# Layer 1's experts in pairs with their weights applied before the last matrix, and layer 3's matrices loaded during the edge loop

## The chip, the cores and the metric

The kernel runs on one core of a Trainium2 chip. The metric is the time of one execution on the device in microseconds (us). The engines are PE (matrix products; PEld is its loading of the stationary operand), DVE, ACT and POOL for element work, and SP, which only issues transfers; ACT and POOL issue transfers as well, each on a queue of its own.

## What is computed

The program is a graph network of four layers on 3125 nodes with 256 features and 103,125 edges. Each layer adds a graph attention, a linear attention and then a feed-forward block to x. The change touches two feed-forward blocks. Layer 1 has a shared network of three matrices and four experts of three matrices, of which the two best count for a node:

```
xn = layernorm(x)
shared = relu(relu(xn @ sW1 + sb1) @ sW2 + sb2) @ sW3 + sb3      # 256 -> 256 -> 128 -> 256
for e in 4 experts:
    o[e] = relu(relu(xn @ eW1[e] + eb1[e]) @ eW2[e] + eb2[e]) @ eW3[e] + eb3[e]   # 256 -> 128 -> 64 -> 256
wf = weights of the top 2 of softmax(xn @ gW + gb), 0 elsewhere
x = x + shared + sum over e of wf[:, e] * o[e]
```

Layer 3 sends each node to one of eight experts: a common hidden layer of 1024 (W1, gelu), a gate on it, and then the matrix Wd[e] (1024 x 256) of the best expert, with bias bd[e], times its probability, added to x.

## The kernel before

Nodes lie in 25 tiles of 125 (TP); a group is four or three tiles (GROUPS: four groups of 4, three of 3), so a product has 500 or 375 columns. All values are float32. The Tile framework orders the instructions on each engine and gives out the buffers of each pool; only in the blocks under `manual_schedule` are PE and DVE kept in the order written. `self.mm(p, pairs)` adds up products in one PSUM tile; since it is a helper, its products are line 716 whatever they compute, and the names of the tiles tell them apart.

**Layer 1, `ffn1`.** `before(i)` transposes a group's xn to xT (line 288), computes the four gate scores (p_score) and the weights wf by `softmax` and `top2`, and is called one group ahead. For a group the kernel computes the shared network (s1 and s2 into p_tr, then for each tile p_y = h2 with s3, plus a product of one row with the bias sb3) and adds it to x on DVE (line 1060). For each expert, e1 goes into p_tr and ACT makes h1e from it (line 1065), e2 into p_e, 64 rows high, and ACT makes h2e (line 1069). Then for each tile a product with e3 goes into p_y, and DVE multiplies it by the node's weight and adds it to x (line 1073). At the end `add_weighted_biases` transposes wf tile by tile (line 707), copies it (709), multiplies it by the biases eb3 (711) and adds (712). p_tr, p_e and p_y have two buffers each.

**Layer 3.** `edge_attention` is a loop of 101 steps of eight columns of 128 edges. In a step SP loads row, ef and mask for two steps ahead, POOL gathers eight times 128 rows into z_edge (line 1930, three buffers), DVE and ACT compute the weights, and PE sums them up (p_acc, line 1998). Twice in a step `piece()` takes one piece of other work from a list: first all pieces of `mix3` (the linear attention, which reads xn and xT), then those of `hidden3`, one generator for each entry of ENDS once the node tiles of that entry are done. `hidden3` writes the hidden layer, the probability and x to hid_d in DRAM. After the loop `routed3` loads w_d, 8 MB, with eight transfers on SP (line 2234), and the biases on ACT's queue (line 2281), sorts the nodes by expert (`route`), and in 32 steps gathers 128 rows of hid_d (hid_tile, line 2244), transposes them, multiplies them by the expert's matrix (p_q, whose address is a register), and scatters the result (line 2412). `routed3`'s tiles use the memory of the loop's and of `hidden3`'s weights.

Of the kernel before, what the change touches and what calls it, by code (L numbers as in the profile page):

```python
# [10 lines left out]
F32 = mybir.dt.float32  # L11
# [4 lines left out]
AF = mybir.ActivationFunctionType  # L16
OP = mybir.AluOpType
# [4 lines left out]
P = 128  # L22
N = 3125
TP = 125
NT = N // TP
C = 256
KC = C // P
# [25 lines left out]
def dview(ap, offset, dims):  # L53
    return bass.AP(tensor=ap.tensor, offset=ap.offset + offset, ap=[list(d) for d in dims])


class Net:
# [950 lines left out]
    def ffn1_weights(self, c):  # L1008
        nc = self.nc
        E = 4  # L1010
        s1, s2, s3 = (self.weight(c, f"L1_ffn_sW{i}", rows=r) for i, r in ((1, 256), (2, 256), (3, 128)))
        sb1, sb2 = self.vec(c, "L1_ffn_sb1"), self.vec(c, "L1_ffn_sb2", rows=P)
        sb3 = self.row(c, "L1_ffn_sb3", parts=1)
        e1 = self.experts(c, "L1_ffn_eW1", E, C)
        e2 = self.experts(c, "L1_ffn_eW2", E, P)
        e3 = self.experts(c, "L1_ffn_eW3", E, 64)
        eb1, eb2 = self.vecs(c, "L1_ffn_eb1", E, P), self.vecs(c, "L1_ffn_eb2", E, 64)
        eb3 = c.tile([E, C], F32, name="eb3")
        nc.sync.dma_start(eb3, self.ins["L1_ffn_eb3"])
        gw, gb = self.weight(c, "L1_ffn_gW"), self.row(c, "L1_ffn_gb")  # L1020
        return s1, s2, s3, sb1, sb2, sb3, e1, e2, e3, eb1, eb2, eb3, gw, gb

    def ffn1(self, x, xn, xT, weights):
        nc, tc = self.nc, self.tc
        E = 4
        with ExitStack() as s:
            c = s.enter_context(tc.tile_pool(name="f1", bufs=1))
            w = s.enter_context(tc.tile_pool(name="f1w", bufs=2))
            wr = s.enter_context(tc.tile_pool(name="f1r", bufs=3))
            ps = s.enter_context(tc.tile_pool(name="f1p", bufs=2, space=PSUM))  # L1030
            s1, s2, s3, sb1, sb2, sb3, e1, e2, e3, eb1, eb2, eb3, gw, gb = weights
            wfs = {}

            def before(i):
                if i < len(GROUPS):
                    t0, nt = g = GROUPS[i]
                    self.transposed(ps, xT, xn, groups=[g])
                    wfs[i] = self.top2(wr, self.softmax(wr, self.scores(wr, ps, xT[:, :, t0 * TP:(t0 + nt) * TP], nt, gw, gb)))

            for g in GROUPS:  # L1040
                self.layernorm(xn, x, g)
            before(0)
            for i, (t0, nt) in enumerate(GROUPS):
                before(i + 1)
                wf = wfs[i]
                n = nt * TP
                cs = slice(t0 * TP, t0 * TP + n)
                h1 = w.tile([P, KC, 512], F32, name="h1")
                for m in range(KC):
                    p = ps.tile([P, 512], F32, name="p_tr")  # L1050
                    self.mm(p[:, :n], [(s1[:, k, m * P:(m + 1) * P], xT[:, k, cs]) for k in range(KC)])
                    nc.scalar.activation(h1[:, m, :n], p[:, :n], AF.Relu, bias=sb1[:, m:m + 1], scale=1.0)
                h2 = w.tile([P, 512], F32, name="h2")
                p = ps.tile([P, 512], F32, name="p_tr")
                self.mm(p[:, :n], [(s2[:, k, :], h1[:, k, :n]) for k in range(KC)])
                nc.scalar.activation(h2[:, :n], p[:, :n], AF.Relu, bias=sb2[:, 0:1], scale=1.0)
                for t in range(nt):
                    q = ps.tile([TP, C], F32, name="p_y")
                    self.mm(q, [(h2[:, t * TP:(t + 1) * TP], s3[:, 0, :]), (self.ones[:1, :TP], sb3)])
                    nc.vector.tensor_add(x[:, t0 + t, :], x[:, t0 + t, :], q)  # L1060
                for e in range(E):
                    p = ps.tile([P, 512], F32, name="p_tr")
                    self.mm(p[:, :n], [(e1[:, e, k, :], xT[:, k, cs]) for k in range(KC)])
                    h1e = w.tile([P, 512], F32, name="h1e")
                    nc.scalar.activation(h1e[:, :n], p[:, :n], AF.Relu, bias=eb1[:, e, :], scale=1.0)
                    p = ps.tile([64, 512], F32, name="p_e")
                    self.mm(p[:, :n], [(e2[:, e, 0, :], h1e[:, :n])])
                    h2e = w.tile([64, 512], F32, name="h2e")
                    nc.scalar.activation(h2e[:, :n], p[:, :n], AF.Relu, bias=eb2[:, e, :], scale=1.0)
                    for t in range(nt):  # L1070
                        q = ps.tile([TP, C], F32, name="p_y")
                        self.mm(q, [(h2e[:, t * TP:(t + 1) * TP], e3[:, e, 0, :])])
                        nc.vector.scalar_tensor_tensor(x[:, t0 + t, :], q, wf[:, t, e:e + 1], x[:, t0 + t, :],
                                                       op0=OP.mult, op1=OP.add)
                self.add_weighted_biases(w, ps, x[:, t0:t0 + nt, :], wf, eb3)

# [250 lines left out]
class Dense(Net):  # L1327
# [831 lines left out]
    def hidden3(self, w, ps, x, xn, xT, t0, nt, weights, ones, hid_d):  # L2159


        nc = self.nc
        E, F = 8, 8
        w1, b1, wg, bg = weights
        n = nt * TP
        cs = slice(t0 * TP, t0 * TP + n)
# [6 lines left out]
        nc.scalar.activation(rstd, mv[:, :, 1], AF.Sqrt, bias=self.eps5[:TP], scale=1.0)  # L2173
        nc.vector.reciprocal(rstd, rstd)
        for t in range(nt):
            nc.vector.tensor_scalar(xn[:, t0 + t, :], x[:, t0 + t, :], mv[:, t, 0:1], rstd[:, t:t + 1],
                                    op0=OP.subtract, op1=OP.mult)
        yield
        for k in range(KC):
            p = ps.tile([P, 512], F32, name="p_h")  # L2180
            for t in range(nt):
                nc.tensor.transpose(p[:, t * TP:(t + 1) * TP], xn[:, t0 + t, k * P:(k + 1) * P], self.ident[:TP, :TP])
            nc.scalar.activation(xT[:, k, cs], p[:, :n], AF.Copy)
            yield
        h = w.tile([P, F, 3 * TP], F32, name="h")
        for f in range(F):
            p = ps.tile([P, 512], F32, name="p_h")
            self.mm(p[:, :n], [(w1[:, k, f * P:(f + 1) * P], xT[:, k, cs]) for k in range(KC)])
# [33 lines left out]
    def routed3(self, ones, hid_d, out):  # L2222

# [5 lines left out]
        y_d = self.dram.tile([N + NJ * P, C], F32, name="y_d")  # L2229
        with ExitStack() as s:  # L2230
            c = s.enter_context(tc.tile_pool(name="r3", bufs=1))
            wd = c.tile([P, F, E, C], F32, name="w_d")
            for e in range(E):
                nc.sync.dma_start(wd[:, :, e, :], self.ins["L3_ffn_Wd"][e].rearrange("(k p) f -> p k f", p=P))
            bd = self.matrix_rows(c, "L3_ffn_bd")
            node, to, mats = self.route(c, ones, NJ)
            wd2 = wd.rearrange("p k e f -> p k (e f)")
# [181 lines left out]
    def run(self, x_in, out):  # L2419
# [17 lines left out]
    def layers(self, x, xn, xT, out):  # L2437
# [32 lines left out]
        with tc.tile_pool(name="layer3", bufs=1) as lp:  # L2470
            ones = lp.tile([TP, NT, 8], BF16, name="one_e")
            hid_d = self.dram.tile([N, HID + 1 + C], F32, name="hid_d")
            with tc.tile_pool(name="edges", bufs=1) as ep:
                with tc.tile_pool(name="ffn2", bufs=1) as wp:
                    weights = self.ffn2_weights(wp)
# [3 lines left out]
                    self.ffn2(x, xn, xT, weights)  # L2479
                self.begin_layer(x, xn, xT)  # L2480
                self.edge_attention(
                    x, xT, edge, lambda w, ps: self.mix3(w, ps, x, xn, xT, mix),
                    lambda w, ps, t0, nt: self.hidden3(w, ps, x, xn, xT, t0, nt, hid, ones, hid_d))
            self.routed3(ones, hid_d, out)

    def general(self, x, xn, xT, out):

# [125 lines left out]
```

## Time and profile before

| | |
|---|---|
| time, median of 3 runs | 5581.91 us (5577.47 to 5591.57) |
| profiled execution | 5581.36 us, span 5579.3 us |
| busy in the span | PE 88%, DVE 68%, ACT 19%, POOL 19% |
| mean granted PE clock | 0.935 |
| layer 1's experts and shared network | 2690 to 2955 us |
| edge loop of layer 3 | 4300 to 5360 us |
| last matrix of layer 3 | 5380 to 5560 us |

The span runs from the first to the last instruction. A line of a timeline gives the start, the length, the engine, the line, the operation, output<-inputs, the number of instructions, and in brackets how long the engine had been idle before and what ended that. A line of the costliest groups gives the busy time and the mean duration in ns, and after the second bar the idle time before and its releaser.

### The profile page before, as it was taken

The numbers are of one execution on the slowest core, as the hardware profiler recorded it, in microseconds if no ns is written. First come the engines' busy times: TensorE is split into PE (matmuls) and PEld (weight loads), VectorE is DVE, ScalarE is ACT, GpSimd is POOL, SyncE is SP. The second block draws the span as 40 slices with busy tenths as digits, with TensorE's granted clock in tenths as the row PEclk, the third lists the DMA queues.
The fourth block names the chain that finished last, engine by engine and source line by source line (L and its number), as shares of the span: only waits on it lengthen the run. The fifth ranks groups of instructions, "written<-read, shape, count | busy, mean of one in ns | idle before, by whom it ended". The sixth has DMA issues, their size and how long they took to land. (4 is left out here: it accounts for less than half of the span.)

```text
span 5579.3 us, 66975 instructions
## 1 busy us (share of the span) xinstructions
PE 4887.1 (88%) x24880; PEld 2854.4 (51%) x24880; DVE 3778.7 (68%) x6022; ACT 1037.5 (19%) x1991; POOL 1038.3 (19%) x1184
## 2 busy tenths in 40 slices
PE   3978888879698899999999899979998888988868
PEld 2652234448555433378544433345565556655557
DVE  7789999975555699745443899932223888777743
ACT  2540010011143100100123000023233112332221
POOL 1000000004200000000001100000001777767733
PEclk7989999979899999999889999979999889999989
DMA  3462222232300011111000011120002556666655
GB/s 87 35 69 66 77 63 66 67 114 65 111 1 1 29 34 41 30 41 36 19 1 4 28 33 34 33 63 0 1 0 65 158 156 179 180 167 169 179 168 170
DMA packets 294389, 395.84 MB, mean 71 GB/s; under 512 B 124223, under 2 KB 228048, under 8 KB 293483
## 3 DMA queue, kind: packets, MB, share of 16 engines
q1 hardware_dynamic: 205646, 163.34, 12.5%
q0 software_dynamic: 52528, 167.17, 10.6%
q10 hardware_dynamic: 35882, 60.93, 3.4%
q8 instruction: 203, 3.33, 0.3%
q14 instruction: 130, 1.06, 0.1%
HBM read 345.14 MB, written 49.35 MB: 71 GB/s over the span
## 5 line engine op out<-in xcount | busy, mean ns | idle before, releaser
L1675 DVE SCALAR_TENSOR_TENSOR pt<-q_head,bar,a 128x750 f32<-128x750 f32 (+5 forms) x1200 | 1483.5, 1299 | 80.3 <-PE acc L1780 57.3
L1930 POOL DMA_INDIRECT z_edge<-tab,src_i x806 | 775.0, 962 | 274.5 <-issue 207.9
L1724 PE MATMUL acc<-pt,zs 128*64 128x500 f32 (+2 forms) x2800 | 592.1, 549 | 150.7 <-DVE pt L1675 126.7
L1775 PE MATMUL acc<-pt,zs 128*64 128x375 f32 (+2 forms) x3200 | 605.9, 502 | 25.2 <-DVE pt L1675 24.9
L1998 PE MATMUL p_acc<-z_edge,oh 128*125 128x264 f32 x2044 | 542.4, 427 | 94.9 <-DVE z_edge L1989 94.8
L1998 PEld LDWEIGHTS p_acc<-z_edge,oh 128*125 128x125 f32 x2044 | 421.1, 210 | 195.3 <-DVE z_edge L1989 105.1
L1724 PEld LDWEIGHTS acc<-pt,zs 128*64 128x64 f32 (+1 forms) x2800 | 244.8, 137 | 482.7 <-DVE pt L1675 327.0
L1775 PEld LDWEIGHTS acc<-pt,zs 128*64 128x64 f32 (+1 forms) x3200 | 245.1, 136 | 362.7 <-issue 224.5
L1191 DVE SCALAR_TENSOR_TENSOR x<-p_y,sm,x 125x256 f32<-125x256 f32 x200 | 93.9, 484 | 428.2 <-PE p_y L716 428.2
L1780 PE MATMUL acc<-pt,zs 128*32 128x375 f32 (+2 forms) x3200 | 313.4, 497 | 0.0
L1826 PE MATMUL acc<-zs,pt 128*125 128x257 f32 x1250 | 275.7, 383 | 11.6 <-issue 11.6
L1826 PEld LDWEIGHTS acc<-zs,pt 128*125 128x125 f32 x1250 | 234.8, 189 | 52.5 <-issue 14.4
L1989 DVE TENSOR_TENSOR z_edge<-z_edge,near_e 128x2112 f32<-128x2112 f32 (+1 forms) x101 | 236.6, 2342 | 16.7 <-ACT near_e L1981 16.7
L1186 ACT ACTIVATE h<-p_tr,bn 128x500 f32<-128x500 f32 (+1 forms) x224 | 161.5, 722 | 361.1 <-PE p_tr L716 361.1
L716 PE MATMUL p_y<-w_L_ffn_Wo,h 128*125 128x256 f32 x800 | 203.7, 387 | 0.0
L1675 DVE SCALAR_TENSOR_TENSOR pt<-q_all,bar,a 128x500 f32<-128x500 f32 (+3 forms) x175 | 119.1, 682 | 122.6 <-PE acc L1826 120.3
L1622 POOL MEMSET es<- 128x4 f32 (+2 forms) x4 | 1.6, 400 | 1052.1 <-PE acc L1780 723.3
L716 PE MATMUL p_tr<-h,w_L_ffn_W 128*128 128x500 f32 (+1 forms) x448 | 191.7, 551 | 6.3 <-ACT h L1186 3.2
L716 PE MATMUL p_tr<-xT,w_L_ffn_W 128*128 128x500 f32 (+1 forms) x448 | 193.0, 554 | 0.0
L2315 POOL CAST one_e<-one 125x96 bf16<-125x96 f32 (+1 forms) x2 | 2.1, 1047 | 1014.0 <-DVE one L653 1014.0
L1780 PEld LDWEIGHTS acc<-pt,zs 128*32 128x32 f32 (+1 forms) x3200 | 85.0, 109 | 203.1 <-issue 201.8
L716 PEld LDWEIGHTS p_y<-w_L_ffn_Wo,h 128*125 128x125 f32 x800 | 144.9, 187 | 73.5 <-ACT h L1186 27.1
(505 smaller groups left out, 6998.5 us busy)
## 6 DMA issues: line engine op xcount, KB each, us to landing
row<-dst_row SPq DMA_DIRECT2D x101, 224.0 KB
a<-count_d SPq DMA_DIRECT2D x96, 203.1 KB
a<-count_d SPq DMA_DIRECT2D x96, 187.5 KB
a<-count_d SPq DMA_DIRECT2D x144, 93.8 KB
ef<-in_edge_s SPq DMA_DIRECT2D x101, 128.0 KB
z_edge<-tab,src_i POOLq DMA_INDIRECT x806
count_d<-stage SPq DMA_DIRECT2D x12, 781.2 KB
q_head<-q_g ACTq DMA_DIRECT2D x24, 375.0 KB
```

What stands on the lines that cost most here:

```text
L716: self.nc.tensor.matmul(p, a, b, start=(i == 0), stop=(i == len(pairs) - 1))
L1186: nc.scalar.activation(o[:, m, :n], p[:, :n], AF.Relu, bias=b[:, e, m:m + 1], scale=g[:, e, m:m + 1])
L1191: nc.vector.scalar_tensor_tensor(x[:, t0 + t, :], q, wf[:, t, e:e + 1], x[:, t0 + t, :], op0=OP.mult, op1=OP.add)
L1675: self.nc.vector.scalar_tensor_tensor(pt[:K, :n], q, bar, a[:K, :n], op0=OP.max, op1=OP.mult)
L1724: nc.tensor.matmul(acc[64 * i:64 * i + 64, :b1 - b0], zs[:K, t, z:z + 64], pts[i][:K, b0:b1], start=(t == 0), stop=(t == NS - 1))
L1775: nc.tensor.matmul(acc[i // 2][64 * (i % 2):64 * (i % 2) + 64, b, :b1 - b0], zs[:K, t, i * W:i * W + 64], pts[i][:K, b0:b1], **st)
L1780: nc.tensor.matmul(acc[2][32 * i:32 * i + 32, b, :b1 - b0], zs[:K, t, z:z + 32], pts[i][:K, b0:b1], **st)
L1826: nc.tensor.matmul(acc[i], pt[:K, i * TP:(i + 1) * TP], zs[:K, t, :C + 1], start=(t == 0), stop=(t == NS - 1))
L1930: nc.gpsimd.indirect_dma_start(out=zs[i][:, j, :], out_offset=None, in_=table, in_offset=bass.IndirectOffsetOnAxis(ap=src[:, c0 + j:c0 + j ...
L1989: nc.vector.tensor_mul(zh, zh, weight[:, :, :, None].to_broadcast([P, n, H, D + 1]))
L1998: nc.tensor.matmul(acc[t], ohs[i, t][:, k - a, :], zs[i][:, k - c0, :HW], start=(k == cols[t][0]), stop=(k == cols[t][1] - 1))
L2315: nc.gpsimd.tensor_copy(ones[:, 0, ts, :], one1)
```

## The change

In layer 1, the experts are taken two at a time. The e2 products of a pair go into the two halves of one PSUM tile of 128 rows, and one Relu gives the tile `pair`. The weights wf, with a column of ones, are transposed in `before` for the whole group (wf_t, five rows). A product of the constant matrix `own` with wf_t gives g, in which each of the 64 rows of an expert holds that expert's weight for each node; DVE multiplies pair by g. The last product of a tile then adds up in one PSUM tile: h2 with s3, the two pairs with e3 (two experts' matrices on 128 rows), and wf_t with the five rows of biases b3. DVE adds the sum to x, once for each tile.

In layer 3, w_d is held by the eight slices f of the hidden layer instead of by the experts. Five of them lie in xT and xn and are loaded on SP's queue by `pieces3`, which follows the pieces of `mix3` in the loop's list with one transfer in every second piece. The other three are loaded by `routed3` where the eight transfers were, by ACT (f = 5 and 7) and SP (f = 6). `hidden3` no longer uses a place in xn and xT for each node tile but one room for three tiles.

```diff
@@ ffn1_weights
-        sb3 = self.row(c, "L1_ffn_sb3", parts=1)
         e1 = self.experts(c, "L1_ffn_eW1", E, C)
         e2 = self.experts(c, "L1_ffn_eW2", E, P)
-        e3 = self.experts(c, "L1_ffn_eW3", E, 64)
-        eb1, eb2 = self.vecs(c, "L1_ffn_eb1", E, P), self.vecs(c, "L1_ffn_eb2", E, 64)
-        eb3 = c.tile([E, C], F32, name="eb3")
-        nc.sync.dma_start(eb3, self.ins["L1_ffn_eb3"])
+        eb1 = self.vecs(c, "L1_ffn_eb1", E, P)
+        e3 = c.tile([P, E // 2, C], F32, name="e3")
+        nc.scalar.dma_start(e3, self.ins["L1_ffn_eW3"].rearrange("(j i) p f -> (i p) j f", i=2))
+        eb2 = c.tile([P, E // 2], F32, name="eb2")
+        with nc.allow_non_contiguous_dma("256 words"):
+            nc.scalar.dma_start(eb2, dview(self.ins["L1_ffn_eb2"], 0, [[1, P], [P, E // 2]]))
+        b3 = c.tile([E + 1, C], F32, name="b3")
+        nc.sync.dma_start(b3[:E], self.ins["L1_ffn_eb3"])
+        nc.sync.dma_start(b3[E:], dview(self.ins["L1_ffn_sb3"], 0, [[0, 1], [1, C]]))
+        own = c.tile([E + 1, E // 2, 2, 64], F32, name="own")
+        nc.gpsimd.iota(own, pattern=[[2, E // 2], [1, 2], [0, 64]], base=0, channel_multiplier=-1, allow_small_or_imprecise_dtypes=True)
+        nc.vector.tensor_scalar(own, own, 0.0, None, op0=OP.is_equal)
+        own = own.rearrange("e j i p -> e j (i p)")
@@ ffn1, before(i)
-                    wfs[i] = self.top2(...)
+                    wf = self.top2(...)
+                    more = wr.tile([TP, nt, E + 1], F32, name="wf_1")
+                    nc.vector.memset(more[:, :, E:], 1.0)
+                    nc.vector.tensor_copy(more[:, :, :E], wf)
+                    p = ps.tile([P, 512], F32, name="p_tr")[:E + 1]
+                    for t in range(nt):
+                        nc.tensor.transpose(p[:, t * TP:(t + 1) * TP], more[:, t, :], self.ident[:TP, :TP])
+                    wfs[i] = wr.tile([E + 1, 512], F32, name="wf_t")
+                    nc.scalar.activation(wfs[i][:, :nt * TP], p[:, :nt * TP], AF.Copy)
@@ ffn1, a group
+                pairs = []
+                for j in range(E // 2):
+                    hs = []
+                    for e in (2 * j, 2 * j + 1):
+                        p = ps.tile([P, 512], F32, name="p_tr")
+                        self.mm(p[:, :n], [(e1[:, e, k, :], xT[:, k, cs]) for k in range(KC)])
+                        hs.append(w.tile([P, 512], F32, name="h1e"))
+                        nc.scalar.activation(hs[-1][:, :n], p[:, :n], AF.Relu, bias=eb1[:, e, :], scale=1.0)
+                    g = ps.tile([P, 512], F32, name="p_e")
+                    nc.tensor.matmul(g[:, :n], own[:, j, :], wf[:, :n], start=True, stop=True)
+                    p = ps.tile([P, 512], F32, name="p_e")
+                    for i2, h in enumerate(hs):
+                        nc.tensor.matmul(p[64 * i2:64 * i2 + 64, :n], e2[:, 2 * j + i2, 0, :], h[:, :n], start=True, stop=True)
+                    pair = w.tile([P, 512], F32, name=f"pair{j}")
+                    nc.scalar.activation(pair[:, :n], p[:, :n], AF.Relu, bias=eb2[:, j:j + 1], scale=1.0)
+                    nc.vector.tensor_mul(pair[:, :n], pair[:, :n], g[:, :n])
+                    pairs.append(pair)
                 for t in range(nt):
+                    ts = slice(t * TP, (t + 1) * TP)
                     q = ps.tile([TP, C], F32, name="p_y")
-                    self.mm(q, [(h2[:, t * TP:(t + 1) * TP], s3[:, 0, :]), (self.ones[:1, :TP], sb3)])
+                    self.mm(q, [(h2[:, ts], s3[:, 0, :])] + [(pairs[j][:, ts], e3[:, j, :]) for j in range(E // 2)] + [(wf[:, ts], b3)])
                     nc.vector.tensor_add(x[:, t0 + t, :], x[:, t0 + t, :], q)
-                for e in range(E):
...
-                self.add_weighted_biases(w, ps, x[:, t0:t0 + nt, :], wf, eb3)
@@ layer 3
+    def room3(self, xT):
+        a, b = xT.rearrange("p k n -> p (k n)"), self.xn_all.rearrange("p t c -> p (t c)")
+        Q = 8 * C
+        parts = [a[:, i * Q:(i + 1) * Q] for i in range(3)] + [b[:, i * Q:(i + 1) * Q] for i in range(2)]
+        norm = b[:TP, 2 * Q:2 * Q + 3 * C].rearrange("p (t c) -> p t c", c=C)
+        turned = b[:, 2 * Q + 3 * C:2 * Q + 3 * C + KC * 3 * TP].rearrange("p (k n) -> p k n", k=KC)
+        return parts, norm, turned
+    def part3(self, queue, out, f):
+        queue.dma_start(out.rearrange("p (e c) -> p e c", c=C), self.ins["L3_ffn_Wd"][:, f * P:(f + 1) * P, :].rearrange("e p c -> p e c"))
+    def pieces3(self, w, ps, x, xn, xT, mix, parts):
+        yield from self.mix3(w, ps, x, xn, xT, mix)
+        for f, o in enumerate(parts):
+            self.part3(self.nc.sync, o, f)
+            yield
+            yield
@@ hidden3 (xn and xT are now the room: norm and turned)
-            nc.vector.tensor_scalar(xn[:, t0 + t, :], x[:, t0 + t, :], mv[:, t, 0:1], rstd[:, t:t + 1],
+            nc.vector.tensor_scalar(xn[:, t, :], x[:, t0 + t, :], mv[:, t, 0:1], rstd[:, t:t + 1],
...
@@ routed3
-            wd = c.tile([P, F, E, C], F32, name="w_d")
-            for e in range(E):
-                nc.sync.dma_start(wd[:, :, e, :], self.ins["L3_ffn_Wd"][e].rearrange("(k p) f -> p k f", p=P))
+            more = c.tile([P, F - len(parts), E * C], F32, name="w_d")
+            wd = list(parts)
+            for f in range(len(parts), F):
+                wd.append(more[:, f - len(parts), :])
+                self.part3(nc.scalar if f % 2 else nc.sync, wd[f], f)
...
-                self.mm(q, [(hts[j][:, f, :], wd2[:, f, bass.ds(mat[j], C)]) for f in range(F)])
+                self.mm(q, [(hts[j][:, f, :], wd[f][:, bass.ds(mat[j], C)]) for f in range(F)])
@@ run
-        xn = pool.tile([TP, NT, C], F32, name="xn")
+        self.xn_all = pool.tile([P, NT, C], F32, name="xn")
+        xn = self.xn_all[:TP]
```

More of the change, by code (lines that the diff above doesn't have):

```diff
@@ L1012, in ffn1_weights @@
         sb1, sb2 = self.vec(c, "L1_ffn_sb1"), self.vec(c, "L1_ffn_sb2", rows=P)
-        sb3 = self.row(c, "L1_ffn_sb3", parts=1)
         e1 = self.experts(c, "L1_ffn_eW1", E, C)
         e2 = self.experts(c, "L1_ffn_eW2", E, P)
-        e3 = self.experts(c, "L1_ffn_eW3", E, 64)
-        eb1, eb2 = self.vecs(c, "L1_ffn_eb1", E, P), self.vecs(c, "L1_ffn_eb2", E, 64)
-        eb3 = c.tile([E, C], F32, name="eb3")
-        nc.sync.dma_start(eb3, self.ins["L1_ffn_eb3"])
+        eb1 = self.vecs(c, "L1_ffn_eb1", E, P)
[11 more added lines that the diff above has]
+        own = own.rearrange("e j i p -> e j (i p)")
         gw, gb = self.weight(c, "L1_ffn_gW"), self.row(c, "L1_ffn_gb")
-        return s1, s2, s3, sb1, sb2, sb3, e1, e2, e3, eb1, eb2, eb3, gw, gb
+        return s1, s2, s3, sb1, sb2, e1, e2, e3, eb1, eb2, b3, own, gw, gb
     def ffn1(self, x, xn, xT, weights):
@@ L1030, in ffn1 @@
             ps = s.enter_context(tc.tile_pool(name="f1p", bufs=2, space=PSUM))
-            s1, s2, s3, sb1, sb2, sb3, e1, e2, e3, eb1, eb2, eb3, gw, gb = weights
+            s1, s2, s3, sb1, sb2, e1, e2, e3, eb1, eb2, b3, own, gw, gb = weights
             wfs = {}
@@ L1037, in before @@
                     self.transposed(ps, xT, xn, groups=[g])
-                    wfs[i] = self.top2(wr, self.softmax(wr, self.scores(wr, ps, xT[:, :, t0 * TP:(t0 + nt) * TP], nt, gw, gb)))
+                    wf = self.top2(wr, self.softmax(wr, self.scores(wr, ps, xT[:, :, t0 * TP:(t0 + nt) * TP], nt, gw, gb)))
+                    more = wr.tile([TP, nt, E + 1], F32, name="wf_1")
[6 more added lines that the diff above has]
+                    nc.scalar.activation(wfs[i][:, :nt * TP], p[:, :nt * TP], AF.Copy)
             for g in GROUPS:
@@ L1057, in ffn1 @@
                 for t in range(nt):
+                    ts = slice(t * TP, (t + 1) * TP)
                     q = ps.tile([TP, C], F32, name="p_y")
-                    self.mm(q, [(h2[:, t * TP:(t + 1) * TP], s3[:, 0, :]), (self.ones[:1, :TP], sb3)])
+                    self.mm(q, [(h2[:, ts], s3[:, 0, :])] + [(pairs[j][:, ts], e3[:, j, :]) for j in range(E // 2)] + [(wf[:, ts], b3)])
                     nc.vector.tensor_add(x[:, t0 + t, :], x[:, t0 + t, :], q)
-                for e in range(E):
[L1062 to L1074, printed above, removed]
@@ L2157, in route3_weights, with hidden3 @@
         return w1, b1, self.weight(c, "L3_ffn_Wg", rows=1024), self.row(c, "L3_ffn_bg")
-    def hidden3(self, w, ps, x, xn, xT, t0, nt, weights, ones, hid_d):
+    def room3(self, xT):
[13 more added lines that the diff above has]
+            yield
+    def hidden3(self, w, ps, x, room, t0, nt, weights, ones, hid_d):
         nc = self.nc
@@ L2165, in hidden3 @@
         n = nt * TP
-        cs = slice(t0 * TP, t0 * TP + n)
+        _, xn, xT = room
         mv = w.tile([TP, nt, 2], F32, name="mv")
@@ L2181, in hidden3 @@
             for t in range(nt):
-                nc.tensor.transpose(p[:, t * TP:(t + 1) * TP], xn[:, t0 + t, k * P:(k + 1) * P], self.ident[:TP, :TP])
-            nc.scalar.activation(xT[:, k, cs], p[:, :n], AF.Copy)
+                nc.tensor.transpose(p[:, t * TP:(t + 1) * TP], xn[:, t, k * P:(k + 1) * P], self.ident[:TP, :TP])
+            nc.scalar.activation(xT[:, k, :n], p[:, :n], AF.Copy)
             yield
@@ L2187, in hidden3 @@
             p = ps.tile([P, 512], F32, name="p_h")
-            self.mm(p[:, :n], [(w1[:, k, f * P:(f + 1) * P], xT[:, k, cs]) for k in range(KC)])
+            self.mm(p[:, :n], [(w1[:, k, f * P:(f + 1) * P], xT[:, k, :n]) for k in range(KC)])
             nc.scalar.activation(h[:, f, :n], p[:, :n], AF.Gelu, bias=b1[:, f:f + 1], scale=1.0)
@@ L2220, in hidden3, with routed3 @@
                 yield
-    def routed3(self, ones, hid_d, out):
+    def routed3(self, ones, hid_d, parts, out):
         nc, tc = self.nc, self.tc
@@ L2231, in routed3 @@
             c = s.enter_context(tc.tile_pool(name="r3", bufs=1))
-            wd = c.tile([P, F, E, C], F32, name="w_d")
-            for e in range(E):
-                nc.sync.dma_start(wd[:, :, e, :], self.ins["L3_ffn_Wd"][e].rearrange("(k p) f -> p k f", p=P))
+            more = c.tile([P, F - len(parts), E * C], F32, name="w_d")
[3 more added lines that the diff above has]
+                self.part3(nc.scalar if f % 2 else nc.sync, wd[f], f)
             bd = self.matrix_rows(c, "L3_ffn_bd")
             node, to, mats = self.route(c, ones, NJ)
-            wd2 = wd.rearrange("p k e f -> p k (e f)")
             w = s.enter_context(tc.tile_pool(name="r3x", bufs=3))
@@ L2472, in layers @@
             hid_d = self.dram.tile([N, HID + 1 + C], F32, name="hid_d")
+            room = self.room3(xT)
             with tc.tile_pool(name="edges", bufs=1) as ep:
@@ L2481, in layers @@
                 self.edge_attention(
-                    x, xT, edge, lambda w, ps: self.mix3(w, ps, x, xn, xT, mix),
-                    lambda w, ps, t0, nt: self.hidden3(w, ps, x, xn, xT, t0, nt, hid, ones, hid_d))
-            self.routed3(ones, hid_d, out)
+                    x, xT, edge, lambda w, ps: self.pieces3(w, ps, x, xn, xT, mix, room[0]),
+                    lambda w, ps, t0, nt: self.hidden3(w, ps, x, room, t0, nt, hid, ones, hid_d))
+            self.routed3(ones, hid_d, room[0], out)
     def general(self, x, xn, xT, out):
```

## The prediction

> **What bounds the kernel now.** 0.3% of the time, about what a measurement of this kernel can tell from no change, is 17 us. The sum is made against the profiled execution: 5581.4 us, span 5579.3; the median of the three runs is 5581.9, so its time stands for them.
>
> I read first the engine table by stretches for the two places that the change touches, layer 1's experts (2690 to 2955 us) and the routed products of layer 3 (5380 to 5480). Columns: stretch, length, then PE, PEld, DVE, ACT, POOL busy, granted clock, DMA share, GB/s.
>
> ```profile
> 2690.00:2955.00 265.00, 261.35 (x765) 125.73 (x766) 117.02 (x438) 70.57 (x115) 0.57 (x2) 0.87 0.01 4
> 5380.00:5400.00 20.00, 5.02 (x39) 4.35 (x37) 11.88 (x53) 3.85 (x8) 0.00 (x0) 0.66 0.98 339
> 5400.00:5420.00 20.00, 5.58 (x20) 4.45 (x21) 1.38 (x2) 1.19 (x2) 3.87 (x4) 0.59 0.90 316
> 5480.00:5500.00 20.00, 20.00 (x114) 17.89 (x113) 7.87 (x15) 2.99 (x5) 8.45 (x10) 1.00 0.56 178
> ```
>
> The experts are bound by PE: 261 of 265 us; DVE (117) and ACT (71) have room. Layer 3 has 40 us in which PE does 10.6 and the DMA engines are full, then a loop that PE fills.
>
> Second, the timeline of weight loads shows when PE takes each product (an fp32 product is two passes).
>
> ```profile
> 2749.87 0.29 PEld L716 LDWEIGHTS p_y<-w_L_ffn_sW,h 128*125 128x125 f32 x2 [0.33 <-issue]
> 2750.50 0.29 PEld L716 LDWEIGHTS p_y<-r_L_ffn_sb,ones 1*125 1x125 f32 x2 [0.33 <-issue]
> ...
> 2754.15 0.19 PEld L716 LDWEIGHTS p_tr<-xT,w_L_ffn_eW 128*128 128x128 f32 x1 [0.23 <-issue]
> 2754.57 0.19 PEld L716 LDWEIGHTS p_tr<-xT,w_L_ffn_eW 128*128 128x128 f32 x1 [0.23 <-issue]
> 2755.55 0.19 PEld L716 LDWEIGHTS p_e<-h1e,w_L_ffn_eW 128*64 128x64 f32 x2 [0.80 <-ACT h1e L1065]
> 2756.53 0.30 PEld L716 LDWEIGHTS p_tr<-xT,w_L_ffn_eW 128*128 128x128 f32 x2 [0.79 <-issue]
> 2757.57 0.72 PEld L716 LDWEIGHTS p_y<-w_L_ffn_eW,h2e 64*125 64x125 f32 x4 [0.74 <-ACT h2e L1069]
> 2758.63 0.19 PEld L716 LDWEIGHTS p_e<-h1e,w_L_ffn_eW 128*64 128x64 f32 x2 [0.33 <-ACT h1e L1065]
> ```
>
> A pass of 500 columns takes 0.42 us, so a product 0.84. Each change of operand shape adds 0.2: p_e 0.98, p_tr between others 1.04, two p_y of 256 columns 1.06 instead of 0.86, a p_y in the alternation with the one-row bias 0.625 instead of 0.43. Two products in different column halves run together: in layer 0 the pairs of 128*64 take 2.96 us for 1625 columns of each of two heads, 0.91 per 500 of both.
>
> ```profile
> 999.88 2.96 PE L1724 MATMUL acc<-pt,zs 128*64 128x500 f32 x16 [0.68 <-DVE pt L1675]
> ```
>
> **Layer 1, PE.** Per group of four tiles (n=500) the change removes: 8 shared p_y with bias, 8 x 0.625 = 5.0; 16 expert p_y, 8 x 1.06 = 8.5; 4 bias p_y of add_weighted_biases, 4 x 0.62 = 2.5; 4 p_e, 3.9; about five breaks of the e1 products by those p_y, 1.0. Sum 20.9. It adds: 4 p_y chains of four products in PSUM, 4 x (4 x 0.43 + 2 changes of shape) = 8.5; two pairs of e2, 2 x 1.04 = 2.1; two products with own, five rows deep, 2 x 1.04 = 2.1. Sum 12.7, net -8.2. A group of three tiles (n=375, product 0.63) likewise: 16.4 out, 9.7 in, -6.7. Four and three groups: -52.9. The 25 transposes of the weights stay, moved to before(). New wait: the last pair needs Relu (0.68) and the multiplication by g (no row; nearest are the 500-column PSUM copy 0.68 and the Relu 0.68; I take 0.7, ends 0.5 and 1.0), with handovers 1.8 us, of which the chain's first two products hide 0.9; behind it on PE stand the rest of the chain and the next group. 7 x 1 = +7. **-46**.
> DVE falls (46.1 + 10.4 us of accumulations become 14 multiplications, 10) and ACT falls (28 half-height Relus, 17.6, become 14, plus 7 copies), so neither takes over.
>
> The clock: the mean 0.87 costs 34 of the 265 us. It falls while PE is recorded busy:
>
> ```profile
> 2735.00:2737.50 2.50, 2.50 (x11) 1.84 (x10) 1.35 (x4) 1.34 (x2) 0.00 (x0) 0.50 0.00 0
> 2740.00:2742.50 2.50, 2.50 (x11) 2.32 (x11) 0.45 (x5) 0.12 (x1) 0.00 (x0) 0.50 0.00 0
> ```
>
> There PE does the transposes of xn and the 4-column scores, which stay. I take the loss as unchanged; ends: all 34 gone, or 10 more. The Trainium skill, "TensorE: Matmul & The Clock Gate", Part 1, lets the clock fall after an idle window of about 3.4 us; these rows show it at half with no idle at all, so by that rule alone a busy PE would lose nothing (total 5492), and the row decides. The same page, Part 4, says that transposes do not count as busy in the same way; that speaks against putting the weights' transposes beside those of xn, and by it 1.1 us a group more at half clock would add an estimated 4 us. I leave it out.
>
> The weights: ACT loses three DMA issues (two of e3, the row sb3, 0.26 to 0.4 each) and gains one, ahead of gwt_g1b (2356.17), for which PE then waits; POOL gains one iota (0.15 to 0.5) and DVE one comparison (0.2). -1 to +1: 0. The loads start 340 us ahead of use; only if that lead went would they show.
>
> **Layer 3.** The end of the chain of work, in the timeline:
>
> ```profile
> 5379.54 23.34 SPq L2234 DMA_DIRECT2D w_d<-in_L_ffn_Wd  x8
> ...
> 5380.02 1.28 ACT L683 ACT_TABLE_LOAD   x1 [1.19 <-DVE sm L682]
> ...
> 5395.72 0.18 DVE L2148 CAST node_of<-at_n 128x32 int32<-128x32 f32 x1
> ...
> 5401.95 1.03 POOL L2244 DMA_INDIRECT hid_tile<-hid_d,node_of  x1 [36.19 <-DMA w_d<-in_L_ffn_Wd]
> ...
> 5418.31 6.55 PE L716 MATMUL p_q<-w_d,hid_t 128*128 x16 [4.56 <-DMA w_d<-in_L_ffn_Wd]
> ```
>
> Eight MB start at 5379.5 (their memory is held until the score's addition), the last hid_d rows and the gather queue among them, and the first product waits until 5418.3. With 3 MB left at 380 GB/s the transfers end near 5391. Next late is node_of: gather at 5396.2 at the earliest, landing some 3 us later (z_edge's take 2.65 to 4), transposes and copies 2.5: first product 5402, -16. But ACT now issues two of the loads (f = 5, 7) ahead of the bias rows, the softmax's Exp (5380.02) and the hid_d copies. SP's second such issue stalled:
>
> ```profile
> 5380.62 5.74 SPq L2234 DMA_DIRECT2D w_d<-in_L_ffn_Wd  x1
> ```
>
> If ACT stalls alike, Exp, one_e, route and gather come 6 to 7 later: first product 5409, -9. Its one load there now, m_L_ffn_bd, goes out at 5379.62, ahead of Exp, so I take it that f = 5 and 7 will too, and lean to the stall: **-11** (ends -5 and -17). The loop after it is PE's own (20.00 of 20.00) and does not change.
>
> Five MB move into the edge loop, on SP's queue. POOL paces that loop, by the costliest groups and by a stretch:
>
> ```profile
> L1930 POOL DMA_INDIRECT z_edge<-tab,src_i x806 | 775.0, 962 | 274.5 <-issue 207.9
> ```
>
> ```profile
> 4610.00:4710.00 100.00, 90.23 (x522) 62.06 (x521) 77.33 (x120) 21.98 (x39) 75.22 (x80) 0.97 0.62 170
> ```
>
> 80 gathers in 100 us is 1.25 each, POOL's full rate, where the parts would load (mix3 has 69 pieces, two a step, and hidden3 starts at 4661); DMA is at 0.62. A MB at full rate is 2.9 us (23.3 / 8); z_edge has three buffers, some 6 us of slack, and SP's row, ef and mask are loaded two steps ahead, so a stalled SP issue (5.7) is covered. If that cover is gone each part costs up to 5.7, 29 in all. I take **+2**. The ten new yields delay hidden3 by five steps: 69 + 118 + 10 = 197 pieces against 206 places before the last group, so nothing is left over; if all ten were, at 1.9 us each (13 pieces in the 24 us after 5361), +19. The shared xn and xT room is rewritten 13 pieces after its last reader: 0; without that distance one normalisation a group, 9 x 1.2.
>
> Sum: -46 - 11 + 2 = -55, from 5581.9: **5527 us**.
>
> **Rivals.** (a) Slower: the weights' transposes take one of two p_tr buffers that the group's first products need, and PE sits out the weights' chain in each group. Price: from the score (2742.0) to the weights (2747.8) 5.9 us, transposes 1.1, copy 0.7, and after such a gap a half-clock spell, 34/7 = 5: 12.7 x 7 = +89, total 5616. It decides from 7.9 us a group on (55/7). For it: two buffers only. Against: the weights are asked for a group ahead, and now transposes of xn already slip in between the bias sums (2733.96). (b) The half-clock spells go with the four-row bias products that precede them: up to -34 more, some 5500. (c) Layer 3 gives nothing back and the loop pays 10 to 29: 5546 to 5565. (d) The pairs run one after the other: 14 x 0.8 = +11, 5538, inside the forecast's own 5508 to 5546.
>
> **Numbers.** Forecast 0.60; (b) 0.15; (c) 0.10; the gains lost to half of (a), no change 0.08; (a) 0.07. Faster 0.85, same 0.08, slower 0.07. The range 5492 to 5566 takes in the forecast, (c) and two thirds of (b).
>
> **What would show it.** Right: the experts' stretch near 219 us with PE still full, p_y in chains of about 2.1 us, e2 pairs near 1 us, the first w_d product 22 to 30 us after the first of the last w_d loads is issued (now 38.8), POOL's gathers still at 1.25. Wrong: PE idle before p_tr with wf_t or one as releaser; pairs of 2 us; POOL waits over 2 us where the five parts load; ACT's Exp not moved by its two loads.

## The result, and the profile after

The changed kernel takes 5539.3 us (median of 4 runs, 5533.5 to 5543.6) against 5586.7 for the kernel before (4 runs): a ratio of 0.9916, 95% interval 0.9901 to 0.9932, so 47 us faster (38 to 55). Run a second time, on a chip on which the edge loop takes as long, it is at 0.9909 (0.9894 to 0.9924), 5536.2 against 5587.4. The profiled execution has a span of 5531.5 us against 5579.3.

Some comparisons below ran on two other chips, on which the edge loop takes 1325 to 1351 us instead of 1040 to 1048, with either layer 3, and the whole kernel some 5% longer; they are called the long-loop chips. Times are therefore compared within one chip only, and stretches away from the loop are read from the profiles.

Cut at the same events, the first two profiles differ like this (us):

| stretch | before | after | difference |
|---|---|---|---|
| start to the experts' first score | 2688.4 | 2683.9 | -4.5 |
| the experts: first score to the next layer's first transposes | 266.1 | 244.0 | -22.1 |
| from there to the first gather of the edge loop | 1345.2 | 1340.5 | -4.7 |
| first to last gather | 1048.0 | 1043.4 | -4.6 |
| last gather to the issue of the last w_d loads | 31.8 | 32.2 | +0.4 |
| that issue to the first scatter of y_tile | 46.6 | 34.0 | -12.6 |
| the rest | 153.2 | 153.4 | +0.2 |

Two rows hold 34.7 of the 47.8 us. The experts gave half of what was forecast. The engine table by stretches for them (columns as before: length, then PE, PEld, DVE, ACT and POOL busy, granted clock, DMA share, GB/s), before:

```profile
2688.38:2954.44 266.06, 262.41 (x771) 126.79 (x770) 117.85 (x440) 70.77 (x116) 0.07 (x1) 0.87 0.02 6
```

and after, with two cuts out of one group:

```profile
2683.92:2927.90 243.98, 202.43 (x649) 104.73 (x648) 73.21 (x317) 67.01 (x109) 0.44 (x2) 0.84 0.02 6
...
2740.00:2742.50 2.50, 0.00 (x0) 0.00 (x0) 2.26 (x12) 0.00 (x0) 0.00 (x0) 0.54 0.00 0
2745.00:2747.50 2.50, 2.50 (x7) 1.35 (x6) 0.06 (x1) 0.58 (x1) 0.00 (x0) 0.50 0.00 0
```

PE is no longer full: 262.4 busy of 266.1 became 202.4 of 244.0, and the idle time rose from 3.6 to 41.6 us. In the cut from 2740 PE does nothing, DVE runs twelve small instructions, and the clock is going down to half, at which PE then starts again. The waits of PE in the stretch name the releaser (us in total, times, longest):

```profile
PE p_tr L1056 <- DVE wf L1053: 40.5, 7, 6.3
```

One wait for each of the seven groups, all at the transposes of the weights (L1056). The timeline of one group shows who stands behind them:

```profile
2738.90 0.17 DVE L698 TENSOR_TENSOR score<-p_score,r_L_ffn_gb 125x16 f32<-125x16 f32 x1 [2.19 <-PE p_score L716]
2744.53 0.18 DVE L1053 COPY wf<-one 125x16 f32<-125x16 f32 x1
2744.85 0.99 PE L1056 MATMUL p_tr<-ident,wf 125*5 125x125 f32 x4 [5.99 <-DVE wf L1053]
2745.64 5.07 PE L716 MATMUL p_tr<-xT,w_L_ffn_sW 128*128 128x500 f32 x6
```

From the score to the weights DVE and ACT take 5.8 us, as before. But now PE sits out this chain, and the shared products of the group in hand (L716, p_tr from xT and sW), which need nothing from it, come only after the transposes. It is the wait that the prediction named as rival (a).

Time lost to the clock, summed over cuts of 2 us as (1 - granted clock) x length, was 34.0 us before and is 38.4 after. The part of it that falls on busy PE went from 33.7 to 20.8, since half-clock time now also lies in the idle gaps. So the stretch can be divided into idle time (+37.9), clock lost on busy PE (-12.9) and what is left, busy time at full clock (228.7 to 181.6, -47.1); together -22.1.

Of the two pairs of e2 products in a group, only the second ran together. In a group of four tiles:

```profile
2756.70 1.95 PE L1090 MATMUL p_e<-h1e,w_L_ffn_eW 128*64 128x500 f32 x4
2763.16 1.06 PE L1090 MATMUL p_e<-h1e,w_L_ffn_eW 128*64 128x500 f32 x4
```

Ahead of the second pair stands the product with own, 1.1 us; ahead of the first it has long been done, and the pair's second product starts 0.89 us after the first, once ACT has made its h1e (2756.70 and 2757.59). In a group of three tiles an e1 product comes between the two products of the first pair (2864.10 and 2865.70). All seven first pairs take 1.7 to 1.95 us and the second ones 0.85 or 1.06, some 6 us more in the stretch.

Layer 3's tail, in the timeline after:

```profile
5344.08 0.40 SPq L2195 DMA_DIRECT2D w_d<-in_L_ffn_Wd  x1
5344.13 0.43 ACTq L2195 DMA_DIRECT2D w_d<-in_L_ffn_Wd  x1
5344.60 1.28 ACT L683 ACT_TABLE_LOAD   x1 [1.18 <-DVE sm L682]
...
5352.32 0.40 ACTq L2195 DMA_DIRECT2D w_d<-in_L_ffn_Wd  x1
5360.45 0.18 DVE L2172 CAST node_of<-at_n 128x32 int32<-128x32 f32 x1
5361.67 1.03 POOL L2291 DMA_INDIRECT hid_tile<-hid_d,node_of  x1 [31.50 <-DMA m_L_ffn_bd<-in_L_ffn_bd]
...
5366.44 1.94 PE L2297 MATMUL p_t<-ident,hid_tile 128*128 128x128 f32 x8 [6.69 <-DMA hid_tile<-hid_d,node_of]
5369.24 1.94 PE L2297 MATMUL p_t<-ident,hid_tile 128*128 128x128 f32 x8 [0.87 <-DMA hid_tile<-hid_d,node_of]
5371.05 2.92 PE L716 MATMUL p_q<-xT,hid_t 128*128 x6
```

Of ACT's two loads only f = 5 goes out ahead of the softmax; f = 7 comes 8.2 us later, behind hid_d rows. The table load for Exp starts 0.52 us after the first load (0.48 before): ACT did not stall. The gather follows node_of by 1.2 us instead of 6.2, and the first product comes 27.0 us after the loads instead of 38.8. It no longer waits for w_d but for the route's own chain, at half clock (the columns are those of the engine table):

```profile
5354.00:5364.00 10.00, 3.17 (x25) 3.03 (x25) 4.70 (x15) 0.00 (x0) 1.98 (x2) 0.50 0.77 242
5364.00:5374.00 10.00, 6.70 (x23) 5.56 (x24) 1.39 (x2) 1.19 (x2) 1.89 (x2) 0.50 0.70 255
```

### The profile page after: what moved, and what is told of

It reads as the page before. It is cut to its first block, busy times and chain, and to the rows that moved or that the text cites. A ratio compares the mean times of both kernels' runs of the same rounds, so it can differ in the third digit from the quotient of the medians.

```text
span 5531.5 us, 66568 instructions
## 1 busy us (share of the span) xinstructions
PE 4813.9 (87%) x24758; PEld 2824.0 (51%) x24758; DVE 3733.4 (67%) x5901; ACT 1034.3 (19%) x1984; POOL 1041.6 (19%) x1185
## 3 DMA queue, kind: packets, MB, share of 16 engines
q1 hardware_dynamic: 203408, 161.12, 12.7%
q0 software_dynamic: 52528, 167.17, 10.7%
q14 instruction: 129, 1.06, 0.1%
## 5 line engine op out<-in xcount | busy, mean ns | idle before, releaser
L1850 PE MATMUL acc<-zs,pt 128*125 128x257 f32 x1250 | 275.7, 383 | 11.8 <-DMA a<-count_d 11.8
L716 PE MATMUL p_y<-w_L_ffn_Wo,h 128*125 128x256 f32 x800 | 203.7, 387 | 0.0
L716 PE MATMUL p_tr<-h,w_L_ffn_W 128*128 128x500 f32 (+1 forms) x448 | 191.6, 551 | 7.8 <-ACT h L1210 4.7
L716 PE MATMUL p_tr<-xT,w_L_ffn_W 128*128 128x500 f32 (+1 forms) x448 | 190.0, 547 | 0.0
L716 PEld LDWEIGHTS p_y<-w_L_ffn_Wo,h 128*125 128x125 f32 x800 | 144.9, 187 | 73.4 <-ACT h L1210 27.1
L1967 DVE TENSOR_TENSOR hot<-row,near 125x1024 f32<-125x1024 int16 (+1 forms) x149 | 157.6, 1083 | 4.5 <-DMA row<-dst_row 2.9
```

The lines of the kernel that those rows point to most:

```text
L716: self.nc.tensor.matmul(p, a, b, start=(i == 0), stop=(i == len(pairs) - 1))
L1850: nc.tensor.matmul(acc[i], pt[:K, i * TP:(i + 1) * TP], zs[:K, t, :C + 1], start=(t == 0), stop=(t == NS - 1))
L1967: nc.vector.tensor_tensor(hots[i, t][:, q0 * 256:q1 * 256], rows[i][:, q0 * 256:q1 * 256], node[:, t:t + 1].to_broadcast([TP, (q1 - q0) * ...
```

## Experiments

**The two halves alone.** The new ffn1 with before's layer 3, and the new layer 3 with before's ffn1, both on one of the long-loop chips:

```
experts_only:  ffn1_weights, ffn1      as changed;  layer 3 as before
layer3_only:   ffn1_weights, ffn1      as before;   layer 3 as changed
```

> The new layer 1 with the old layer 3. In the profiles the stretch of layer 1's experts (first score to last sum) went from 266.1 to 244.0 us, -22.1, and layer 3's tail (issue of the last w_d loads to the first scatter) from 46.6 to 34.0, -12.6; the other 13 us fell in stretches with the same work (4.5 ahead of the experts, 4.7 after them, 4.6 in the edge loop). Theory 1: these 13 us are spread from run to run, so this kernel is at before minus 22, 5560 to 5566. Theory 2: the experts' half also brings the 9 us around it, so 5550 to 5556. The stretch itself 244 with 42 us of idle PE under both.

> The old layer 1 with the new layer 3. Theory 1 (tail alone): before minus 12.6, 5571 to 5576, and the edge loop (first to last gather, 1048.0 before, 1043.4 after) within 5 us of 1048. Theory 2: the loop gains from the edit too, and the kernel is at minus 17, near 5569, with a loop of 1043. The prediction's own terms give -9.

Experts alone: 0.9925 of before (0.9906 to 0.9944), 33 to 55 us. Layer 3 alone: 0.9959 (0.9944 to 0.9974), 15 to 33 us. Both gains lie above the number of theory 1, but on this chip the loop alone differs by up to 25 us between profiles of kernels with the new layer 3 (1325.4 to 1350.6), so the totals decide nothing here. The stretches do. The experts take 244.2 us in the one and 270.7 in the other; the tail 46.7 in the one and 34.3 in the other. Each half's stretch changes with its own edit and not with the other's:

```profile
2694.00:2938.20 244.20, 202.64 (x648) 104.84 (x648) 73.19 (x317) 67.02 (x109) 0.43 (x2) 0.84 0.02 6
```

That is the experts' stretch of experts_only: busy, idle and clock as in the changed kernel.

**The weights' transposes in a PSUM tile of their own**, on a long-loop chip and on one with the short loop:

```
-                    p = ps.tile([P, 512], F32, name="p_tr")[:E + 1]
+                    p = ps.tile([P, 512], F32, name="p_wf", bufs=1)[:E + 1]
```

> The changed kernel with the transposes of the weights in a PSUM tile of their own (one buffer) instead of p_tr. Theory: the 38 us by which idle PE grew in the experts' stretch come from p_tr's buffers, which are handed out in the program's order: the shared products stand behind the weights' transposes, and these behind DVE's top-2 chain. With a tile of their own the shared products go first; the idle falls from 42 to about 4 us, the stretch from 244 to 206 if the time lost to the half clock stays at 38, up to 219 if more of it now falls on busy PE. Total 5501 to 5514. Rival: PE waits for something else there (the copy of wf_t, own products), and the time stays within 5 us of 5539.

> The changed kernel with the weights' transposes in a PSUM tile of their own, beside the changed kernel on one chip. Theory: 244.0 less the 193.3 us that its stretch took in the first run of it, so 46 to 55 us under the changed kernel, of which some 40 are idle PE and 10 the clock. Rival: some of that was the other chip's; then less than 40.

> The changed kernel itself, as the yardstick for the runs beside it. In the earlier comparison it was 0.9916 of before. Theory: the experts' stretch 244 us with 42 of idle PE again, the tail (w_d issue to first scatter) 34, so 0.990 to 0.994 of before; what differs elsewhere between two profiles (some 5 us ahead of the experts, 5 after, 5 to 20 in the edge loop) is spread.

The first ran on the long-loop chip: 0.9819 of before (0.9799 to 0.984), stretch 193.3 us. The second, beside the changed kernel: 5487.0 us against 5536.2 for the changed kernel and 5587.4 for the one before, 0.9816 of before (0.9803 to 0.9829). That is 49 us under the changed kernel. (The changed kernel's second profile repeats the first: stretch 244.0 us, tail 33.8.) In the profile of own_bank_2, the stretch, then the group of the transposes (busy, mean ns | idle before, releaser), then one group's cut on PE:

```profile
2685.47:2875.63 190.16, 188.73 (x648) 97.16 (x648) 70.73 (x317) 66.16 (x109) 0.43 (x2) 0.96 0.03 8
```

```profile
L1056 PE MATMUL p_wf<-ident,wf 125*5 125x125 f32 x25 | 3.8, 270 | 0.8 <-DVE wf L1053 0.8
```

```profile
2728.50 2.04 PE L716 MATMUL p_tr<-h,w_L_ffn_sW 128*128 128x500 f32 x4
2730.37 2.68 PE L716 MATMUL p_tr<-xT,w_L_ffn_eW 128*128 128x500 f32 x6
2732.89 0.59 PE L1056 MATMUL p_wf<-ident,wf 125*5 125x125 f32 x4
```

The wait went from 40.5 to 0.8 us, the transposes now come behind the shared products and in the middle of the first experts', and the stretch from 244.0 to 190.2. Idle PE gave 40.1 of these 53.8 us, the clock on busy PE 13.2 (20.8 to 7.6). The stretch is shorter than the 206 us expected at best, because the expectation had left the clock's loss where it was. Against the kernel before, the change without this wait takes 75.9 us off the stretch: 47.6 of busy time at full clock, 26.1 of clock on busy PE and 2.2 of idle time.

**A third buffer of p_tr instead:**

```
-    p = ps.tile([P, 512], F32, name="p_tr")            # every p_tr of ffn1
+    p = ps.tile([P, 512], F32, name="p_tr", bufs=3)
```

> The changed kernel with three buffers of p_tr instead of two, the weights' transposes still in p_tr. The prediction's rival (a) blamed the number (two buffers only). Theory 1 (number): with a third buffer the shared products start before the weights are there, and the stretch falls from 244 to some 200. Theory 2 (order): p_tr's buffers are handed out in the order in which the program asks for them, so the shared products still stand behind the transposes on PE: 244 and 42 us of idle PE as with two, and the time of the changed kernel within 5 us.

5541.6 us, 0.992 of before (0.9902 to 0.9938): the changed kernel's time (5539.3 and 5536.2). The stretch is 243.4 us, and the group of the transposes waits as it did:

```profile
L1056 PE MATMUL p_tr<-ident,wf 125*5 125x125 f32 x25 | 6.3, 403 | 39.9 <-DVE wf L1053 33.7 <-issue 6.1
```

So not the number of buffers but their order. The shared products' p_tr is asked for after the transposes' p_tr, and on PE they stay behind them even with a third buffer. A tile name of their own takes them out of that line.

**The half clock on busy PE: before, without its alternation.** The weights are transposed for a group at once; all sums stay as they were:

```
 def before(i):
...
+    p = ps.tile([P, 512], F32, name="p_wf", bufs=1)[:E]
+    for t in range(nt):
+        nc.tensor.transpose(p[:, t * TP:(t + 1) * TP], wfs[i][:, t, :], self.ident[:TP, :TP])
+    wts[i] = wr.tile([E, 512], F32, name="wf_t")
+    nc.scalar.activation(wts[i][:, :nt * TP], p[:, :nt * TP], AF.Copy)
...
-    self.add_weighted_biases(w, ps, x[:, t0:t0 + nt, :], wf, eb3)
+    for t in range(nt):
+        q = ps.tile([TP, C], F32, name="p_y")
+        nc.tensor.matmul(q, wts[i][:, t * TP:(t + 1) * TP], eb3, start=True, stop=True)
+        nc.vector.tensor_add(x[:, t0 + t, :], x[:, t0 + t, :], q)
```

> The kernel before, with one thing changed in layer 1's experts: the weights are transposed for a group together, in a PSUM tile of their own and a group ahead, and copied once, so that the four-row bias products need no transpose, copy and wait of DVE between them; all sums stay as they were. In before 34 us of the stretch of 266 went at the half clock with PE recorded busy; with own bank 11. Theory 1: the half-clock spells follow the short waits in the alternation of transposes, copies and four-row products; without it the loss falls to 10 to 20 us and the stretch to 240 to 250. Theory 2: the spells follow the transposes of xn and the 4-column scores, which stay: 30 to 38 lost, stretch 258 to 266.

0.9963 of before (0.995 to 0.9976), 13 to 28 us, and in the stretch:

```profile
2686.28:2935.47 249.19, 246.78 (x770) 118.01 (x769) 110.18 (x415) 73.81 (x123) 0.06 (x1) 0.92 0.02 6
```

16.9 us shorter than before's, of which some 4 could be spread (before's own stretch is 266.1 us here and 270.3 on a long-loop chip); the clock takes 18.5 us of busy PE instead of 33.7. That is theory 1, and nearly half of the loss goes with this grouping alone. The profile of before shows hardly any of it as idle time. Its waits for wf_t:

```profile
PE p_tr L707 <- DVE wf_t L709: 1.1, 4, 0.3
PE p_y L711 <- DVE wf_t L709: 1.1, 4, 0.3
```

In one group PE stands still for 0.7 us in all, in three pieces between 2728.9 and 2733.4, and the clock falls to half at 2734.4. The Trainium skill, "TensorE: Matmul & The Clock Gate", section "A second HAM failure mode: psum-queue depth-cycling", describes a clock that oscillates because of very short idle times between groups of products that cycle through PSUM. The 15.2 us that came back here fit that, but no run separates the short idle times from the rest of what the grouping changed (the transposes also moved, a group ahead). What makes the remaining 18.5 (a spell at half clock still follows the transposes of xn and the scores, from 2732.2 to 2739.0) no run took apart.

**The parts of w_d late.** Two kernels:

```
late_parts:  pieces3 issues no loads; routed3 issues all five parts on SP, into xT and xn
late_all:    pieces3 issues no loads; self.routed3(ones, hid_d, [], out): eight slices
             into w_d's own tile, four on SP and four on ACT
```

> The changed kernel with the five parts of w_d loaded after the loop, on SP ahead of the other three, into the same places. Theory 1: the tail's gain is that of fewer bytes, so about 12 us come back and the total is 5549 to 5554, the first routed product 36 to 39 us after the first load instead of 27. Theory 2: the gain is that of the split of one matrix per issue into one slice per issue and of the second queue; then less than 5 us come back. The loop without the loads: by the prediction 2 us shorter, by its rival 10 to 29.

> The changed kernel with all eight slices of w_d loaded after the loop, from the score on, four on SP and four on ACT, into w_d's own tile; the five parts are not loaded early. (With the parts only written behind the loop, their loads still went out at 4381 to 4731 us, so that run could not tell.) Theory 1: the tail's 12.3 us are the 5 MB that are no longer in it: the first scatter again 44 to 49 us after the first load instead of 34, and 10 to 15 us more in all. Theory 2: the split into slices, which lets the first product start on the first slice, and the second queue are what gains: 34 to 38, and less than 4 us more.

late_parts could not tell: its profile has the five loads at 4380.9 to 4731.4, inside the loop, as in the changed kernel (4349.6 to 4633.1). Nothing held them back, since their places were free. It came to 0.9896 of before on a long-loop chip, with a tail of 32.4 us. In late_all the loads need memory that the loop still holds. It takes 5546.9 us, 10.7 more than the changed kernel beside it; its tail is 45.1 us and its first product comes 38.9 us after the first load. Its timeline:

```profile
5348.42 9.52 SPq L2195 DMA_DIRECT2D w_d<-in_L_ffn_Wd  x4
...
5362.64 0.60 ACT L2261 ACTIVATE hid_row<-p_h 125x512 f32<-125x512 f32 x1 [9.18 <-DMA w_d<-in_L_ffn_Wd]
...
5364.80 0.18 DVE L2172 CAST node_of<-at_n 128x32 int32<-128x32 f32 x1
...
5373.47 1.03 POOL L2290 DMA_INDIRECT hid_tile<-hid_d,node_of  x1 [39.01 <-DMA w_d<-in_L_ffn_Wd]
```

Theory 1: the tail's gain is the five megabytes that are no longer in it; the slices and the second queue, which late_all has too, give at most 1.5 us of it (46.6 to 45.1). ACT does stall here, for 9.2 us, but behind the softmax: node_of still comes 16.4 us after the first load, as in the changed kernel, and what is late is the gather, 8.7 us after node_of instead of 1.2.

**Each part loaded twice in the loop:**

```
             self.part3(self.nc.sync, o, f)
+            self.part3(self.nc.sync, o, f)
```

> The changed kernel with each of the five parts loaded twice into its place in the edge loop: 10 MB instead of 5. The prediction put the five loads at +2 us in the loop (0 to 29). Theory 1 (covered by the slack of the gathers): 0 to 3 us more than the changed kernel. Theory 2 (each load stops the loop for its own 2.9 to 5.7 us): 15 to 29 more.

5537.4 us against 5536.2. The gathers' groups over the loop, of the changed kernel, of double_parts and of late_all, which loads nothing there:

```profile
L1954 POOL DMA_INDIRECT z_edge<-tab,src_i x806 | 773.8, 960 | 267.7 <-issue 208.3 <-PE p_acc L2022 32.6 <-DVE e L2003 3.4
```

```profile
L1954 POOL DMA_INDIRECT z_edge<-tab,src_i x806 | 774.7, 961 | 267.0 <-issue 208.9 <-PE p_acc L2022 32.0 <-DMA z_edge<-tab,src_i 3.4
```

```profile
L1954 POOL DMA_INDIRECT z_edge<-tab,src_i x806 | 774.9, 961 | 268.4 <-issue 208.6 <-PE p_acc L2022 34.3 <-DVE l L2000 3.7
```

With five, ten and no megabytes on SP it is 1040.0, 1040.3 and 1041.8 us from the first to the last gather. No cost of the loads shows.

**Spread of the stretches that were not touched.** One more profile each of the kernel before and of the new layer 3 alone:

> The kernel before once more, for a second profile of it. Of the 47.8 us between the two first profiles, the experts' stretch (-22.1) and the tail (-12.6) give 34.7; 13 lie in stretches with the same work: 4.5 ahead of the experts, 4.7 from their end to the first gather, 4.6 in the edge loop. Theory 1 (spread): this profile has 1340 to 1346 us between experts and loop and a loop anywhere from 1040 to 1048. Theory 2 (the loop gains from the new layer 3): a loop of 1047 to 1049 again, as in both profiles with the old one (1048.0, 1047.7), against 1040 to 1047 in six with the new one.

> The old layer 1 with the new layer 3, beside that profile. Theory 1: tail 34, experts 266, everything else within 5 us of the kernel before. Theory 2: the loop as well, at 1040 to 1044.

Both ran on a long-loop chip, with loops of 1345.6 and 1333.7 us, so they say nothing of 5 us there. The experts take 270.3 us in both, the tail 47.1 and 33.8. They do say that the time between experts and loop is spread: 1342.9 and 1344.3. Over all profiles with either layer 1 it runs from 1340.3 to 1346.3, and the time ahead of the experts from 2683.9 to 2697.5.

## Why the prediction was right, and where it was not

The total was forecast at 5527, 55 us faster, and came out 47 faster (38 to 55), inside the range. In this there was luck. Its largest term was twice too large, and it was not further off because two things that the sum had put at nothing worked against each other: the wait of rival (a) cost 53.8 us in the stretch, and without it 26.1 us of half clock would have gone, the gain that rival (b) spoke of. About 13 us in stretches that no term named made up for half of what the experts fell short.

- **Layer 1, -46: measured -22.** The products were nearly as counted: -52.9 forecast, -47.1 measured as busy time at full clock. A tile's chain comes every 2.1 us, as forecast (four from 2726.5 to 2734.9). A pair of e2 takes the forecast 1.04 us only the second time in a group (1.06); the first pair's products run one after the other, which is some 6 us, as much as the missing 5.8. Where the product with own stands ahead of the first pair too, in the first group of own_bank_2, both pairs take 1.06. So rival (d) was half right: the sum took it that the operands of both pairs are ready in time, and those of one are.
- **The new wait, +7, was put at the wrong place.** Behind the last pair PE does not wait at all; it does not appear among PE's waits of the stretch. The wait that came is rival (a)'s, at 5.8 us a group (40.5 / 7), 38 us more idle time in all. The prediction had given it 0.07, on the argument that the weights are asked for a group ahead and that transposes of xn already slip in between. The step that failed is that argument: what counts is not how early the weights are asked for but that the products of the group in hand ask for p_tr after them. Two of (a)'s own statements fell too. Its reason, "two buffers only", fell with three_p_tr. Its price of 12.7 a group did not hold either: own_bank_2 puts it at 53.8 / 7 = 7.7, of which 5.7 are idle time and 1.9 half clock on busy PE. The half-clock spell costs less than the 5 that were charged, because a part of each spell lies in the gap itself.
- **The clock, 0 (ends -34 and +10): -12.9 on busy PE**, inside its ends. Rival (b), given 0.15, was right in part: bias_grouped shows 15 us of the 34 hanging on the alternation with the four-row products. In own_bank_2 26.1 of the 33.7 are gone; what took the other 11 was not separated. In the changed kernel 13.2 of these 26.1 went back, because PE starts at half clock after each gap.
- **Layer 3's tail, -11: measured -12.6** (first product -11.8), right by two errors that cancel. The prediction leaned to a stall of ACT that delays Exp and the route by 6 to 7 us. It did not come, not even with 8 MB in the tail (late_all, where ACT stalls for 9.2 us behind Exp). But from the gather to the first product it takes 9.4 us and not the 5.8 that the sum had (5402 less 5396.2): rows(1) stand before products(0) on PE, so the first product also waits for the second tile's rows and transposes, all at a clock of 0.50 (5354 to 5374).
- **The edge loop, +2 (0 to 29): 0 for the loads**, by double_parts and late_all. Rival (c) is out.
- **What no term named, about -13.** The parts of it before and after the experts lie within the spread of those stretches. The loop itself may have become shorter: 1048.0 and 1047.7 in the two profiles with the old layer 3 and the short loop, 1040.0 to 1047.0 in six with the new one or with its loads left to the end. On the long-loop chips the two mix (1326.5 and 1345.6 with the old one, 1325.4 to 1350.6 with the new). It is not the loads, which late_all lacks; whether the later hidden3 groups or the small norm room do it, or whether it is chance, stays open.

## What to carry to other kernels

An engine that works in order pays for a tile name as well as for a product: a transpose that waits for a long chain, written into the same rotating PSUM tile as products that are ready, puts them all behind that chain. Give the late one a name of its own, and look in the waits for one stall in each round of the loop with the same releaser; here that one line was worth as much again as the whole change (49 us). When a price is put on a rival, add up only what its gap adds: here its own length and 1.9 us of half clock, 7.7 us a group instead of 12.7. And a forecast that comes out right can hide two rivals that cancel; only a kernel without the one showed the size of the other. Five megabytes of loads cost nothing that shows in a loop whose DMA engines are busy 0.62 of the time (the kernel before, 4610 to 4710 us), and 10.7 to 12.6 us at the head of the serial tail.

## What the runs showed of the hardware

Two rows of the changed kernel, cut where its clock falls and where it returns (columns as before):

```profile
2740.00:2740.40 0.40, 0.00 (x0) 0.00 (x0) 0.40 (x3) 0.00 (x0) 0.00 (x0) 0.73 0.00 0
2750.40:2750.80 0.40, 0.40 (x2) 0.19 (x1) 0.00 (x0) 0.00 (x0) 0.00 (x0) 0.97 0.00 0
```

- The granted clock fell to half 1.3 us after PE had gone idle (idle from 2738.9, half from 2740.2) and returned 5.6 us after PE began again (2744.8 to 2750.4). The Trainium skill, "TensorE: Matmul & The Clock Gate", Part 1, speaks of an idle window of about 3.4 us; here 1.3 us of recorded idle sufficed, after 2 us of 4-column scores at full clock.
- The half-clock spells that lie wholly in the experts' stretch last 3.4, 6.8, 10.2 or 13.7 us, whole multiples of 3.41, in the four profiles before, after, bias_grouped and own_bank_2. In the changed kernel four of the last five gaps bring a spell of 10.2 us, of which 5.0 to 5.6 fall on busy PE, and one a spell of 6.8, of which 2.7 do.
- Time lost to half speed on a PE that is recorded busy: 33.7 us of the 262 before, 18.5 with the transposes grouped, 7.6 in the changed kernel with its transposes in a tile of their own.
- Two e2 products in different halves of the columns take 1.06 us together (500 columns) where one alone takes 0.98, if both operands are ready; where the second waits for ACT, 1.95.
- 806 gathers went at the same pace beside 0, 5 or 10 MB of loads (1041.8, 1040.0, 1040.3 us).
- Two chips ran the kernel before's edge loop in 1048 and in 1346 us; the experts' stretch differed by 4 us only (266.1 and 270.3). The cause of that was not followed.
